# Roots from the sums, a one-step scale, half stores, unread products and a new order in an attention and quantised-layer kernel

## The chip, the cores and the metric

The kernel runs on one core of one Trainium2 chip. The metric is the device time of one execution in microseconds (us). Everything is float32 at the ends; the kernel uses bfloat16 and an eight-bit float inside.

## The reference, cut to what matters

The input `x` is 16 sequences of 512 tokens with 256 features. Two sandwiched layers follow one another:

```python
h  = layernorm(layernorm(x)) * ln_w + ln_b      # eps 1e-5 in both
q, k, v = h @ w_q, h @ w_k, h @ w_v             # 16 heads of 16
q, k = rope(q, theta), rope(k, theta)
t = qk / 4;  a = 1 + t + t*t/2                  # "Taylor softmax"
wv = (a / a.sum(-1)) @ v                        # every token sees every token
x  = x + layernorm(wv @ w_o)

z  = layernorm(x)
s  = max(max|z| over blocks of 32 / 7.5, 1e-30) # one scale for 32 features
zd = nearest_fp6(z / s) * s                     # the weights likewise, once
x  = x + layernorm(zd @ wd.T + bias)
```

Because the polynomial is of second degree, the attention never forms the 512 x 512 matrix: sums over tokens of products of key features with `v` (the tile `psi` holds the features) are multiplied by the same features of the queries.

## The kernel before, in words

The sequence is the unit of work. For each of the 16 sequences the program records some 195 operations: load (`x_load`), double layernorm (`statistics`, `normalised`), transposition, the products with `wk`, `wv_w` and `wq`, rotary embedding, the key features (`coefficients`: DVE, with sums on GpSimd), the query features (`features`: products and ACT squares), the token sums (`token_sums`, L1341), the attention products (`main_part` L1403 and L1422), a DMA round trip that brings the divisors to their places, the division (L1501, for the last two sequences products with a selector and L1539), the product with `wo`, `residual`, the layernorm before the quantiser (`deviations`), the quantiser (`quantised`), the transposition, the product with `wdT` (to which a bf16 product with the bias rows, L993, is added), a second `residual`, and the store.

Every operation is recorded by a `Plan` with its engine, an assumed cost (the first number of each call) and the tiles that it reads and writes. Nothing is emitted then. At the end the literal tuple `ORDER`, 3317 numbers, says in which order the recorded operations are emitted; this is the order of each engine's list, since an engine takes its instructions in order. The order also hands out the buffers: a tile takes a free slot of its class (27 pages, 8 PSUM banks, and so on) when its first operation comes up and gives it back behind its last. So the sequences overlap as the tuple says. Dependences are kept by semaphores that the framework derives.

Five places matter here.

- **Reciprocal root.** `statistics` (17 uses) and `deviations` (54 uses) need 1/sqrt(v + eps) for two or four columns per partition. Six operations: DVE adds eps (L608), ACT takes the root (L763 or L797), DVE takes the reciprocal (L764 or L798), and one Newton step follows: a product (L618) and two combined operations (L628).
- **Scale in `quantised`.** The largest magnitudes `am` of blocks (L858) are divided by 7.5 with a correction: a tensor-scalar (L606), three combined operations (L628), and the lower limit (L606 again). The reciprocal (L869), the products by it and by the scale (L879), and the rounding to eight bits (ACT, L910) follow. A sequence has 32 columns of scales in one piece; the last two sequences have two halves of 16 columns, with the products on DVE instead of GpSimd (`quick`).
- **Stores.** One DMA of 512 KB per sequence from SP's queue. Those of sequences 12 to 15 are the last four numbers of `ORDER`.
- **Sums of squares.** `deviations` lets ACT square 256 columns and accumulate (L784). Only the assumed cost of these operations is touched.
- **Start.** DVE clears the eight banks (L1606), GpSimd sets ones in the first 128 columns of `bias3` (L1604). The weights' quantiser (`exact`) and the rotary table run on DVE in the first 60 us, among the work of the first sequences.

Of the kernel before, what the change touches and what calls it, by code (L numbers as in the profile page):

```python
# [17 lines left out]
ALU = mybir.AluOpType  # L18
# [82 lines left out]
def constants():  # L101
# [40 lines left out]
    8, 3, 0, 93, 65, 9, 16, 4, 1, 5, 7, 2, 6, 333, 94, 19, 20, 95, 66, 21, 132, 67, 130, 22, 23,  # L142
    24, 133, 131, 134, 13, 14, 135, 17, 10, 25, 96, 26, 136, 137, 138, 139, 27, 28, 29, 146, 31,
    140, 147, 30, 148, 338, 149, 97, 68, 69, 32, 12, 141, 142, 143, 150, 151, 144, 145, 48, 33,
    336, 34, 35, 49, 98, 340, 152, 337, 341, 36, 153, 154, 155, 37, 156, 99, 38, 39, 40, 41, 42,
    70, 339, 334, 11, 157, 158, 50, 51, 43, 44, 335, 45, 53, 52, 100, 54, 71, 162, 159, 160,
    161, 46, 47, 125, 165, 55, 342, 343, 72, 73, 101, 163, 164, 166, 56, 57, 76, 167, 15, 126,
    128, 127, 129, 18, 200, 179, 189, 195, 168, 174, 528, 1503, 918, 723, 919, 202, 203, 204,
    1308, 921, 61, 191, 922, 730, 180, 104, 201, 529, 205, 169, 206, 102, 925, 181, 531, 183,
    182, 1113, 344, 731, 345, 59, 74, 533, 103, 346, 347, 207, 530, 532, 348, 1315, 923, 184,  # L150
    208, 187, 245, 240, 170, 106, 192, 924, 177, 535, 105, 190, 350, 246, 185, 209, 349, 188,
    351, 352, 244, 247, 171, 194, 186, 198, 728, 193, 58, 172, 199, 920, 176, 178, 536, 62, 926,
    175, 173, 107, 726, 78, 196, 108, 534, 197, 109, 537, 724, 110, 353, 355, 220, 242, 354,
    356, 243, 235, 395, 236, 237, 239, 241, 63, 221, 215, 238, 222, 216, 223, 357, 224, 225,
    227, 218, 217, 538, 219, 228, 229, 230, 226, 111, 60, 1116, 79, 112, 539, 540, 541, 542, 75,
    113, 725, 1120, 727, 114, 77, 80, 927, 115, 543, 81, 82, 397, 83, 117, 729, 1510, 210, 231,
    233, 213, 214, 64, 234, 232, 360, 928, 211, 212, 251, 249, 248, 250, 252, 84, 732, 362, 85,
    545, 547, 546, 544, 396, 86, 1118, 361, 359, 358, 87, 374, 550, 399, 398, 1698, 254, 1309,
    253, 255, 256, 400, 548, 257, 258, 1504, 375, 376, 1114, 259, 1313, 401, 402, 1705, 549,
    551, 733, 734, 735, 363, 384, 382, 590, 261, 378, 377, 262, 264, 265, 266, 267, 260, 263,  # L160
    268, 592, 365, 929, 386, 552, 554, 591, 553, 440, 379, 116, 442, 403, 435, 364, 380, 383,
    385, 437, 555, 89, 930, 736, 737, 738, 381, 931, 932, 933, 1699, 394, 366, 387, 741, 436,
    404, 88, 441, 438, 390, 369, 594, 593, 595, 269, 90, 118, 410, 569, 557, 571, 556, 388, 570,
    367, 368, 393, 371, 370, 271, 270, 414, 740, 411, 412, 742, 439, 275, 936, 739, 934, 119,
    120, 430, 572, 573, 745, 433, 272, 746, 432, 273, 431, 274, 577, 743, 598, 91, 578, 434,
    413, 373, 276, 372, 935, 277, 415, 416, 417, 92, 418, 419, 391, 278, 389, 279, 392, 280,
    281, 284, 1703, 285, 283, 422, 423, 579, 585, 558, 574, 282, 744, 420, 596, 937, 288, 421,
    581, 121, 1311, 405, 424, 289, 406, 286, 425, 287, 408, 426, 785, 290, 291, 292, 293, 559,
    566, 294, 1506, 295, 428, 764, 940, 409, 427, 429, 407, 296, 597, 786, 787, 122, 297, 599,
    298, 446, 444, 443, 445, 299, 941, 575, 300, 447, 582, 560, 1115, 568, 301, 766, 302, 303,  # L170
    576, 304, 1121, 305, 789, 788, 564, 790, 635, 450, 448, 449, 451, 938, 939, 637, 750, 636,
    123, 791, 625, 452, 453, 768, 306, 1119, 307, 765, 308, 454, 751, 1117, 561, 563, 792, 310,
    980, 747, 793, 309, 627, 626, 629, 628, 311, 749, 752, 748, 630, 314, 312, 632, 124, 580,
    313, 315, 772, 316, 317, 457, 455, 456, 631, 794, 773, 633, 634, 605, 319, 318, 565, 982,
    1122, 1123, 588, 321, 981, 1508, 606, 586, 584, 460, 459, 767, 458, 769, 770, 462, 461, 463,
    464, 983, 984, 465, 320, 607, 608, 587, 567, 1124, 1125, 562, 322, 323, 583, 589, 324, 771,
    468, 467, 466, 469, 470, 471, 325, 610, 612, 472, 609, 613, 611, 614, 615, 616, 326, 473,
    474, 475, 327, 476, 1126, 1127, 753, 479, 480, 478, 477, 483, 481, 330, 755, 329, 617, 618,
    774, 759, 985, 600, 959, 482, 619, 620, 484, 601, 775, 604, 623, 621, 988, 776, 485, 486,
    1701, 961, 328, 487, 331, 488, 777, 489, 490, 491, 1312, 1128, 960, 602, 624, 622, 962, 963,  # L180
    964, 603, 639, 640, 638, 641, 494, 493, 642, 492, 495, 779, 781, 496, 782, 497, 1310, 1314,
    498, 499, 500, 501, 502, 1130, 1131, 1129, 986, 643, 644, 645, 754, 1132, 646, 989, 503,
# [250 lines left out]
def sandwich_kernel(  # L433
# [1169 lines left out]
    with tc.manual_schedule():  # L1603
        nc.gpsimd.memset(bias3.a[:, 0:P], 1.0)  # L1604
        for slot in plan.slots["bank"]:
            nc.vector.memset(slot, 0.0)  # L1606
# [43 lines left out]
```

## Time and profile before

| | |
|---|---|
| Time, median of 3 runs | 612.54 us (610.73 to 616.55) |
| Profiled execution: own time | 612.84 us |
| its span, first to last instruction | 611.0 us |
| mean granted TensorE clock | 0.985 |
| PE busy, weight loads | 569.1 us, 393.8 us |
| DVE, ACT, GpSimd busy | 531.3, 503.8, 181.3 us |
| DMA | 41.27 MB, 68 GB/s on average |

PE is TensorE's matmuls, PEld its weight loads, DVE VectorE, ACT ScalarE, POOL GpSimd, SP the engine that issues most DMAs. Busy time is the union of the instructions' spans. Matmuls are pipelined and their ends are modelled, so 93% busy on PE is not 93% of its peak. The chain of waits goes back from the last instruction, at each step to what released it or to the instruction before it on its engine; its shares tell what the end of the span hung on. A line such as L628 is a helper: all combined operations of DVE on small tiles carry it, and the shape tells them apart.

### The profile page before, as it was taken

The numbers are of one execution on the slowest core, as the hardware profiler recorded it, in microseconds if no ns is written. First come the engines' busy times: TensorE is split into PE (matmuls) and PEld (weight loads), VectorE is DVE, ScalarE is ACT, GpSimd is POOL, SyncE is SP. The second block draws the span as 40 slices with busy tenths as digits, with TensorE's granted clock in tenths as the row PEclk, the third lists the DMA queues.
The fourth block names the chain that finished last, engine by engine and source line by source line (L and its number), as shares of the span: only waits on it lengthen the run. The fifth ranks groups of instructions, "written<-read, shape, count | busy, mean of one in ns | idle before, by whom it ended". The sixth has DMA issues, their size and how long they took to land.

```text
span 611.0 us, 14678 instructions
## 1 busy us (share of the span) xinstructions
PE 569.1 (93%) x5460; PEld 393.8 (64%) x5460; DVE 531.3 (87%) x1346; ACT 503.8 (82%) x1264; POOL 181.3 (30%) x137
## 2 busy tenths in 40 slices
PE   0869999999999999999999999999999999999964
PEld 0636776777757676767866666776767676765543
DVE  7999998899999989888798999888896968997596
ACT  3566699888898888998988878999988897889973
POOL 2310414334333060613343260333327033430200
PEclk9969999999999999999999999999999999999988
DMA  7420410401223141603124212302114020113103
GB/s 221 141 82 18 109 38 19 94 19 21 52 64 89 55 109 48 185 1 98 33 64 134 70 21 74 94 2 63 32 61 139 11 67 36 41 47 89 25 32 104
DMA packets 34968, 41.27 MB, mean 68 GB/s; under 512 B 9808, under 2 KB 27728, under 8 KB 34896
## 3 DMA queue, kind: packets, MB, share of 16 engines
q1 hardware_dynamic: 33344, 38.88, 23.0%
q10 hardware_dynamic: 1552, 1.44, 0.9%
q8 instruction: 43, 0.70, 0.5%
q14 instruction: 29, 0.24, 0.1%
HBM read 17.90 MB, written 9.31 MB: 45 GB/s over the span
## 4 chain that ended last, share of the span: by engine, by line
PE 75%; DVE 12%; ACT 5%; DMA 4%; issue 2%; SPq 1%; DVEq 0%; ACTq 0%
PE bank L985 32%; PE bank L1403 9%; PE bank L1341 9%; PE bank L1128 7%; PE bank L1289 5%; PE bank L924 5%; PE bank L1422 3%; PE bank L1312 3%; DVE psi L1257 2%; PE bank L1049 2%; ACT page L1279 2%; DMA page<-in_L_attn_x_dram 1%; PE bank L993 1%; ACT page L1437 1%; DVE page L1088 1%
## 5 line engine op out<-in xcount | busy, mean ns | idle before, releaser
L1279 ACT ACTIVATE page<-bank 128x512 f32<-128x512 f32 x256 | 145.5, 612 | 10.5 <-PE bank L1289 9.7
L1257 DVE TENSOR_TENSOR psi<-psi 128x896 f32<-128x896 f32 x128 | 142.0, 1127 | 1.0 <-ACT psi L1201 1.0
L1161 POOL TENSOR_TENSOR half<-half,half 128x512 f32<-128x512 f32 x32 | 46.5, 1453 | 189.9 <-DMA half<-half 108.5
L816 ACT ACTIVATE page<-page,small,small 128x256 f32<-128x256 f32 x128 | 70.6, 600 | 7.8 <-DVE small L628 6.4
L1341 PE MATMUL bank<-psi,va 128*17 128x153 f32 x2048 | 72.0, 294 | 2.0 <-DVE half L1143 0.7
L985 PE MATMUL bank<-wdT,page 128*128 128x256 f32 x256 | 66.7, 392 | 2.1 <-ACT page L1571 1.3
L1341 PEld LDWEIGHTS bank<-psi,va 128*17 128x17 f32 x2048 | 57.6, 98 | 17.1 <-issue 9.1
L1188 POOL TENSOR_TENSOR psi<-page,page 128x512 f32<-128x512 f32 x32 | 44.2, 1388 | 74.7 <-PE bank L1341 60.1
L985 PE MATMUL bank<-wk,page 128*128 128x256 f32 x256 | 63.6, 393 | 1.6 <-ACT page L1037 1.6
L784 ACT ACTIVATE squares_room<-bank 128x256 bf16<-128x256 f32 x128 | 50.2, 393 | 15.6 <-PE bank L993 8.3
L879 POOL TENSOR_TENSOR page<-page,small 128x1024 f32<-128x1024 f32 (+1 forms) x16 | 29.4, 1839 | 113.6 <-DVE small L869 57.2
L1128 PE MATMUL bank<-page,wq 128*128 128x256 f32 x256 | 62.7, 390 | 0.2 <-ACT page L1279 0.2
L985 PE MATMUL bank<-wo,page 128*128 128x256 f32 x256 | 60.0, 384 | 2.9 <-ACT page L1279 1.8
L985 PE MATMUL bank<-wv_w,page 128*128 128x256 f32 x256 | 61.1, 384 | 0.2 <-ACT page L1279 0.2
L1403 PE MATMUL bank<-page,page 128*32 128x512 f32 x512 | 58.5, 595 | 0.0
L1017 DVE SCALAR_TENSOR_TENSOR page<-bank,small,page 128x256 f32<-128x256 f32 x128 | 56.3, 473 | 1.4 <-DVE small L628 0.5
L985 PEld LDWEIGHTS bank<-wk,page 128*128 128x128 f32 x256 | 47.8, 194 | 14.1 <-ACT page L1037 2.4
L1128 PEld LDWEIGHTS bank<-page,wq 128*128 128x128 f32 x256 | 47.6, 193 | 13.6 <-issue 2.7
L985 PEld LDWEIGHTS bank<-wo,page 128*128 128x128 f32 x256 | 46.9, 190 | 13.6 <-ACT page L1279 2.6
L985 PEld LDWEIGHTS bank<-wdT,page 128*128 128x128 f32 x256 | 44.9, 194 | 15.2 <-ACT page L972 2.3
L985 PEld LDWEIGHTS bank<-wv_w,page 128*128 128x128 f32 x256 | 46.9, 190 | 10.3 <-issue 2.8
L1289 PE MATMUL bank<-two,sums 32*128 32x512 f32 x512 | 50.7, 451 | 0.4 <-DVE page L1017 0.4
(106 smaller groups left out, 1021.6 us busy)
## 6 DMA issues: line engine op xcount, KB each, us to landing
half<-half SPq DMA_DIRECT2D x64, 128.0 KB
out_dram<-page SPq DMA_DIRECT2D x16, 512.0 KB
page<-in_L_attn_x_dram SPq DMA_DIRECT2D x15, 512.0 KB
page<-rows SPq DMA_DIRECT2D x14, 512.0 KB
page<-page SPq DMA_DIRECT2D x64, 64.0 KB
rows<-rd SPq DMA_DIRECT2D x56, 16.0 KB
page<-in_L_attn_x_dram SPq DMA_DIRECT2D x2, 256.0 KB
rd<-page SPq DMA_DIRECT2D x32, 16.0 KB
```

The lines of the kernel that those rows point to most:

```text
L784: lambda: nc.scalar.activation(squares_room.a, view(src.a), AF.Square, accum_out=sq.a[:, i : i + 1], **known, **({} if mean is None else { ...
L816: lambda: nc.scalar.activation(dst.a[:, first + i], view(src.a), AF.Identity, bias=nb.a[:, i : i + 1], scale=r.a[:, i : i + 1],),
L985: nc.tensor.matmul(pt.a[:, i * D : (i + 1) * D], srcT.a[:, k, c * P : (c + 1) * P], view(k), start=(k == 0), stop=(k == NK - 1 and rows is ...
L1017: lambda: nc.vector.scalar_tensor_tensor(dst.a[:, c], view(src.a), r.a[:, i : i + 1], base.a[:, c], ALU.mult, ALU.add),
L1128: nc.tensor.matmul(pq.a[:, n * D : (n + 1) * D], wq.a[:, k, hf * P : (hf + 1) * P], hT.a[:, k, n * D : (n + 1) * D], start=(k == 0), stop= ...
L1161: lambda: nc.gpsimd.tensor_tensor(cos.a, cos.a, partner.a, ALU.add),
L1188: nc.gpsimd.tensor_tensor(lin().rearrange("p s (i two) -> p s i two", two=2), rc.a[:, hf].rearrange("p c (h i two) -> p (c h) i two", i=HD ...
L1257: nc.vector.tensor_tensor(psi.a[:, s, HD:F_MAIN].rearrange("p s (d i) -> p s d i", i=HD), lin()[:, s].unsqueeze(2).to_broadcast([P, HH, NS ...
L1279: lambda: nc.scalar.activation(dst.a[:, part], pk.a, AF.Square, **bias),
L1289: nc.tensor.matmul(pk[quad].a, sums.a[r, odd], q.a[r, n], start=(n == 0), stop=(n == 1), tile_position=(quad * HS, 0),)
L1341: nc.tensor.matmul(pst.a[j * HS : j * HS + HV, i * F_ALL : (i + 1) * F_ALL], va.a[:, c, (g2 * HH + h8) * HV : (g2 * HH + h8 + 1) * HV], ps ...
L1403: nc.tensor.matmul(banks[g].a[j * HS : (j + 1) * HS], sT.a[:, 0, j, g * HS : (g + 1) * HS], feats[j // 2][0][g % 2, j % 2].a[:, g // 2], s ...
```

## The change

- The reciprocal root becomes a helper `rsqrt`. ACT takes 2 sqrt(v + eps) directly from the variances or sums, with the factor as its scale and a constant tile `eps4` as its bias. DVE computes 4(v + eps) and its reciprocal meanwhile, multiplies by the root, takes the root's reciprocal and adds the two, which is the Newton step's value in another form. Again five DVE operations and one of ACT.
- The quantiser's scale for the sequences is one tensor-scalar (times 1/7.5, lower limit). The weights keep the longer way.
- The stores of the last two sequences go out in halves, each recorded behind its half's residual.
- Twenty groups of six products of ones are recorded on PE (numbers 3247 to 3266). Each writes a bank that nobody reads.
- The assumed costs of the sums of squares are lower (0.472 and 0.602 in place of 0.6 and 0.725).
- `ORDER` is another tuple, with 3267 numbers: 72 operations fewer in the quantiser, two stores and twenty groups more. On PE's list four groups stand ahead of the first transposition; one between the two transpositions of sequence 0, one on either side of its second product with `wv_w`, one behind its first query features, two ahead of its first rest features; then one among sequence 15's features, one behind the transposition of sequence 13's quantised page, one ahead of and two behind the first transposition of sequence 14's, one ahead of its second product with `wdT`, and four behind the last product of sequence 15.

```diff
+    def rsqrt(n, r, name, src, scale, add):
+        v4, inv, sd = (small(f"{name}_{i}", n) for i in ("v4", "inv", "sd"))
+        act(
+            0.205,
+            [V.base(src), eps4],
+            [sd],
+            lambda: nc.scalar.activation(
+                sd.a, V.ap(src), AF.Sqrt, bias=eps4.a[:, add : add + 1], scale=scale
+            ),
+        )
+        V.ts(n, v4, src, scale, 4.0 * EPS * (EPS if add else 1.0), ALU.mult, ALU.add)
+        vec(0.17, [v4], [inv], lambda: nc.vector.reciprocal(inv.a, v4.a))
+        V.tt(n, inv, sd, inv, ALU.mult)
+        vec(0.17, [sd], [v4], lambda: nc.vector.reciprocal(v4.a, sd.a))
+        V.tt(n, r, v4, inv, ALU.add)
...
         if twice:
-            V.ts(n, ve, var, 1.0 + EPS, EPS * EPS, ALU.mult, ALU.add)
+            rsqrt(n, r, "ln", var, 4.0 * (1.0 + EPS), 1)
         else:
-            V.ts(n, ve, var, EPS, None, ALU.add)
-        act(0.205, [ve], [sd], lambda: nc.scalar.activation(sd.a, ve.a, AF.Sqrt))
-        vec(0.17, [sd], [r], lambda: nc.vector.reciprocal(r.a, sd.a))
-
-        V.tt(n, t, r, r, ALU.mult)
-        V.stt(n, t, t, -0.5, ve, ALU.mult, ALU.mult)
-        V.stt(n, r, t, 1.5, r, ALU.add, ALU.mult)
+            rsqrt(n, r, "ln", var, 4.0, 0)
         V.stt(n, nb, mean, -1.0, r, ALU.mult, ALU.mult)
...
-                0.6 if mean is None else 0.725,
+                0.472 if mean is None else 0.602,
...
-        V.ts(n, ve, sq, 1.0 / D, EPS, ALU.mult, ALU.add)
-        act(0.205, [ve], [sd], lambda: nc.scalar.activation(sd.a, ve.a, AF.Sqrt))
-        vec(0.17, [sd], [r], lambda: nc.vector.reciprocal(r.a, sd.a))
-        V.tt(n, t, r, r, ALU.mult)
-        V.stt(n, t, t, -0.5, ve, ALU.mult, ALU.mult)
-        V.stt(n, r, t, 1.5, r, ALU.add, ALU.mult)
+        rsqrt(n, r, "dev", sq, 4.0 / D, 0)
...
-        V.ts(n, s, am, inv, None, ALU.mult)
-        V.stt(n, e, s, -8.0, am, ALU.mult, ALU.add)
-        V.stt(n, e, s, 0.5, e, ALU.mult, ALU.add)
-        V.stt(n, s, e, inv, s, ALU.mult, ALU.add)
-        V.ts(n, s, s, 1e-30, None, ALU.max)
+        if exact:
+            V.ts(n, s, am, inv, None, ALU.mult)
+            V.stt(n, e, s, -8.0, am, ALU.mult, ALU.add)
+            V.stt(n, e, s, 0.5, e, ALU.mult, ALU.add)
+            V.stt(n, s, e, inv, s, ALU.mult, ALU.add)
+            V.ts(n, s, s, 1e-30, None, ALU.max)
+        else:
+            V.ts(n, s, am, inv, 1e-30, ALU.mult, ALU.max)
...
-            residual(y, x2, banks, [2 * c2 + i for c2 in cs for i in range(2)])
-        dma(
-            nc.sync,
-            2.5,
-            [y],
-            [],
-            lambda: out[b].rearrange("(c p) d -> p c d", **kp),
-            lambda: y.a,
-        )
+            cs = [2 * c2 + i for c2 in cs for i in range(2)]
+            residual(y, x2, banks, cs)
+            cut = slice(cs[0], cs[-1] + 1)
+            dma(
+                nc.sync,
+                2.5 if len(cs) == NT else 2.001,
+                [y] if len(cs) == NT else [(y, c) for c in cs],
+                [],
+                lambda cut=cut: out[b].rearrange("(c p) d -> p c d", **kp)[:, cut],
+                lambda cut=cut: y.a[:, cut],
+            )
...
+    ones = bias3
+
+    def warm():
+        pt = bank()
+
+        def emit():
+            row = ones.a[:, 0:P].unsqueeze(1).to_broadcast([P, T // P, P])
+            for _ in range(6):
+                nc.tensor.matmul(
+                    pt.a.rearrange("p (c n) -> p c n", n=P),
+                    ones.a[:, 0:P],
+                    row,
+                    start=True,
+                    stop=True,
+                )
+
+        pe(1.28, [(ones, 0)], [pt], emit)
+
+    for _ in range(20):
+        warm()
+
     with tc.manual_schedule():
         nc.gpsimd.memset(bias3.a[:, 0:P], 1.0)
+        for i in range(2):
+            nc.gpsimd.memset(eps4.a[:, i : i + 1], 4.0 * EPS * (EPS if i else 1.0))
```

The two tuples are left out; the prediction names the places of them that it uses.

## The prediction

> **What bounds the kernel now.** I read the page first: engine totals, clock, chain.
>
> ```profile
> PE 569.1 (93%) x5460; PEld 393.8 (64%) x5460; DVE 531.3 (87%) x1346; ACT 503.8 (82%) x1264; POOL 181.3 (30%) x137
> ...
> PEclk9969999999999999999999999999999999999988
> ...
> PE 75%; DVE 12%; ACT 5%; DMA 4%; issue 2%; SPq 1%; DVEq 0%; ACTq 0%
> ```
>
> Three engines are near full (PE 93%, DVE 87%, ACT 82% of the span), and the chain that ended last passes three quarters of its length through PE. The granted clock is at 9 tenths or more except in the third slice and the last two. So no single engine explains the span: it is PE work plus the places where PE waits. The stretches show where these are.
>
> ```profile
> core 0: us, PE busy (x) PEld busy (x) DVE busy (x) ACT busy (x) POOL busy (x), PEclk, DMA share, GB/s
> 0.00:58.50 58.50, 36.36 (x276) 25.62 (x280) 52.83 (x181) 32.89 (x65) 11.06 (x17) 0.91 0.39 116
> 58.50:553.00 494.50, 490.02 (x4841) 341.22 (x4840) 436.73 (x1008) 428.28 (x1073) 166.38 (x118) 1.00 0.23 62
> 553.00:611.00 58.00, 42.75 (x348) 27.00 (x348) 41.73 (x159) 42.59 (x128) 3.82 (x2) 0.93 0.23 66
> ```
>
> Columns: length, then busy time of PE, PEld, DVE, ACT, POOL with counts, granted clock, DMA. I cut at 58.5 (from here the chain stays mostly on PE) and 553 (from here it leaves it). Adding the chain's pieces by stage gives: **start** 57.8 us, of which PE 14.2 and DVE 26.2, unbroken on DVE from 22.9 to 48.4; **middle** 494.5 us, of which PE 426.6, DVE 35.0, ACT 23.2, DMA 4.4; **tail** 54.1 us, of which PE only 16.9, DVE 14.8, DMA 7.5, ACT 6.9. In the middle the chain is off PE for 68 us, mostly in three passages: 207.7 to 221.1, 325.7 to 358.1 and 483.4 to 497.7. DVE is busy 12.98 of 13.4 us in the first and 30.48 of 32.4 in the second. So the start, these passages and 581 to 592 of the tail are where DVE work counts fully; elsewhere it hides behind PE.
>
> **The parts, and what each is worth.** The sum is against the profiled execution's own 612.84 us (span 611.0, 1.84 around it), 0.3 above the median of 612.54 (610.73 to 616.55).
>
> **1. One-step scale.** Each rescale of sequences loses four small DVE operations. The chain of waits passes through one of them at 215.5 (time, us, what):
>
> ```profile
> 215.51 0.69 DVE small L628
> ...
> 216.22 0.20 DVE small L628
> ```
>
> The groups, by shape (busy, mean ns of one, idle before):
>
> ```profile
> L1279 ACT ACTIVATE page<-bank 128x512 f32<-128x512 f32 x256 | 145.5, 612 | 10.5 <-PE bank L1289 9.7
> ...
> L1279 ACT ACTIVATE page<-bank,shift 128x512 f32<-128x512 f32 x64 | 42.8, 699 | 3.2 <-PE bank L1312 3.0
> ...
> L606 DVE TENSOR_SCALAR small<-small 128x32 f32<-128x32 f32 x42 | 8.7, 206 | 0.5
> L628 DVE SCALAR_TENSOR_TENSOR small<-small,small 128x32 f32<-128x32 f32 x42 | 8.5, 202 | 1.0
> ```
>
> With 32 columns: three at 202 ns and one at 206, 0.81 us; fourteen such, 11.3 us. With 16 columns: three at 172 and one at 158, 0.67 us; four, 2.7 us. Only what stands on the chain counts: in the middle two rescales do (215.5, and 354.7 with the same lines), so 2 x 0.81 = **-1.6**. The cover of the other twelve is PE; were DVE to set the pace all through, it would be -11.3. In the tail, where the quantiser's products run on DVE too, the chain lies on DVE almost unbroken; some of the 2.7 is overlap, so **-2.0** (0 to -2.7).
>
> **2. Reciprocal roots.** 71 of them (L763 x17, L797 x54). DVE work stays equal: before, a tensor-scalar 195, reciprocal 172, product 161 and two of L628 at 167 are 0.86 us; after, 195, twice 172, twice 161, again 0.86. What changes is the chain. The timeline of the last one:
>
> ```profile
> 604.67 0.17 DVE L608 TENSOR_SCALAR small<-small 128x2 f32<-128x2 f32 x1
> ...
> 604.87 0.20 ACT L797 ACTIVATE small<-small 128x2 f32<-128x2 f32 x1 [0.23 <-DVE small L608]
> 605.14 0.15 DVE L798 RECIPROCAL small<-small 128x2 f32<-128x2 f32 x1
> 605.33 0.16 DVE L618 TENSOR_TENSOR small<-small 128x2 f32<-128x2 f32 x1
> 605.52 0.36 DVE L628 SCALAR_TENSOR_TENSOR small<-small,small 128x2 f32<-128x2 f32 x2
> 606.34 0.88 DVE L1017 SCALAR_TENSOR_TENSOR page<-bank,small,page 128x256 f32<-128x256 f32 x2 [0.46 <-DVE small L628]
> ```
>
> From the end of the last sum of squares (604.63) to L628's end the steps follow one another: tensor-scalar, root, reciprocal, product, two more. In the change the root starts on ACT's own sums, with no DVE step first, while DVE does v4 and its reciprocal; behind the root come product, reciprocal, sum. From 604.67: root 0.20 plus 0.09 (below), then three steps at the 0.19 by which these starts follow one another, gives 605.6 where it was 605.88: -0.28. About five are in series in the tail (two roots of sequence 14, three of 15): **-1.4** (0 to -3.4, all twelve). In the middle these lines hold about 2 us of the chain, less 22%: **-0.4**. ACT's 8.5 us idle for L608 goes; behind it queue the evictions that free PE's banks. The DVE operation that now waits is the product with the root, with the rest of DVE's list behind it, as L798 waits today (6.2 us).
>
> The root now takes its bias from a tile. No row shows a root both ways; nearest are L1279 with and without a tile bias, 699 and 612 (+87 ns), and L784, 511 and 393 (+118, with another source too). I take 0.09 of 0 to 0.118: 71 x 0.09 = 6.4 us of ACT. ACT has 4.7% of the middle's chain: **+0.3**; if ACT set the pace, +6.4. The Trainium skill, ScalarE: Activation LUTs, section "What ACT_TABLE_LOAD costs", states that each pointer operand adds about 93 ns; by that figure, an estimate, ACT gains 6.6 us and the sum moves by nothing visible.
>
> **3. Stores in halves.** Only the last two sequences. The last 512 KB store issues at 607.25 and the span ends 3.75 later. Half of it goes earlier; the fixed part remains. Gain 0 to 1.9, and two issues more on SP at a median 0.49 each, ahead of the last one if DVE finishes early (at worst +1.0). I take **-0.7**, nearer to no gain, since small stores have a landing time too.
>
> **4. Unread products.** 20 groups of six 512-column bf16 matmuls. The chain shows 256 columns of bf16 (L993) at 0.11 us, so 0.22 each, 1.32 a group, 26.4 in all. By the new list four come ahead of the first transposes, six among the start's products, six in the tail's, and four behind the last real product. PE is busy 36.4 of 58.5 us at the start and 42.8 of 58 in the tail, so 22.1 and 15.3 us of room hide them; where the operands behind a group are already there, it costs its 1.32 whole. Gain: the first eight L985 matmuls take 3.78 us and the same eight later 1.73, but that is ahead of a DVE passage that is full anyway (18.07 of 18.10 from 30.5 to 48.6); in the tail the clock is 0.93 for 42.8 us of PE, 16.9 of it on the chain: 1.2 at most. I take **-0.5** (+21.1 for sixteen groups to -3.2).
> The Trainium skill, TensorE: Matmul & The Clock Gate, section "What's actually happening", says PE starts at half clock and is released after some 3.4 us of activity. Taken by that rule alone the first matmuls would save 2.05 us, and the sum would be 2.05 lower; the 3.78 against 1.73 agrees with the rule, though the granted clock of the stretch from 15.3 to 23 us reads 1.00.
>
> **5. The new order.** Start: ahead of the first token sums the new list leaves out five 256-wide products and one mask of the weights' quantiser (0.43 x3, 0.41 x2, 0.29: 2.4 us) and has four small operations more (0.66): **-1.7**, since DVE is unbroken there. That work comes later, under PE. In the middle a list can open or close passages: the three are 60.1 us together, another like the first would cost 13.4. One thing can be read from the lists: the wait of L1501 for the DMA round trip (9.6 us of DVE idle). Work by the kernel's own costs between the last av product and L1501 is at least 13 us of DVE before and 16 after. I take a third of the 9.6, **-3.0** (+13.4 to -60).
>
> **Sum:** -1.7 -1.6 -2.0 -1.4 -0.4 +0.3 -0.7 -0.5 -3.0 = -11.0, so **601.8 us**, PE remaining the bound.
>
> **Rivals.**
> *A, DVE was the pace-setter.* For: DVE 87%, and two of three passages full of it. Against: the chain has 7% of the middle on it. Then the rescale gives its whole 11.3 instead of 1.6, and L1501's 9.6 go instead of 3.0: 601.8 - 9.7 - 6.6 = 585.5.
> *B, the middle takes nothing.* For: PE alone has 426.6 of 494.5; what DVE saves and the start postpones is met again. Only the tail gains: 612.8 - 2.0 - 1.4 - 0.7 = 608.7.
> *C, ACT sets the pace.* For: 82% busy, its evictions free the banks. Against: 4.7% of the middle's chain. 601.8 - 0.3 + 6.4 = 607.9. The page on ScalarE named above gives the same direction.
> *D, the unread products stand in the way* (slower). Place: PE's list, where six groups lie between products of the start and six in the tail, and PE takes them in order. Each whose followers are ready costs 1.32. For: the two just ahead of sequence 0's rest features feed ACT, and three stand around sequence 14's first turned block. Against: 22.1 and 15.3 us of room. From nine groups on (11.5 / 1.32 = 8.7) the change loses; at all sixteen, 601.8 + 0.5 + 21.1 = 623.4.
>
> **Chances.** My forecast 0.50 (its own range 594 to 607), A 0.18, B 0.14, C 0.06, D 0.12. A measurement of this kernel tells about 1% from no change (606.4 to 618.7). Faster: 0.46 + 0.18 + 0.04 of B + 0.03 of C = 0.71; same: 0.04 + 0.10 + 0.03 + 0.02 of D = 0.19; slower: 0.10. The range goes to A's time and into D: 586 to 617.
>
> **What would show it.** Right: DVE about 14 us less busy (517), L606 and L628 with 32 columns fewer by 14 and 42; root rows near 0.3 us and no ACT wait for a tensor-scalar; token sums of sequence 0 starting near 47 instead of 48.6; the tail beginning (last main products of sequence 15 done) some 6 us sooner; the last store about 3 us before the end; PE busy up by up to 26 while its chain share does not rise. Wrong: PE waits behind groups of ones with data ready (D); ACT pieces growing in the chain (C); the chain off PE in the middle for 68 us still (B) or under 50 (A).

## Result and profile after

The changed kernel takes 607.39 us (median of 17 runs, 604.46 to 609.22), the kernel before, run beside it, 613.30 (17 runs, 609.48 to 616.55): a ratio of 0.9904 (0.9884 to 0.9923). A later comparison of the same pair on one chip, the first of the last four experiments below, gave 606.13 against 614.35, 0.9855 (0.982 to 0.9889). The change is faster by 1.0 to 1.4%, 6 to 9 us, where 11 were forecast. Both intervals exclude no change, though 607.4 by itself lies within the 606.4 to 618.7 that the prediction could not tell from none. The profiled execution took 607.85 us with a span of 605.8.

The page of the profile after: busy times, granted clock in 40 slices, and the shares of the chain that ended last.

```profile
PE 588.0 (97%) x5580; PEld 405.1 (67%) x5580; DVE 534.5 (88%) x1274; ACT 510.1 (84%) x1264; POOL 185.4 (31%) x139
...
PEclk8889999999999999999999999998999999999999
...
PE 69%; DVE 17%; ACT 7%; DMA 3%; issue 2%; POOL 1%; SPq 0%; ACTq 0%; DVEq 0%
```

PE is now busy 97% of the span instead of 93%, but that is the unread products (without them it is 564.6 us, third experiment below, where it was 569.1 before); the chain has less PE on it than before (69%, it was 75) and more DVE (17%, it was 12). DVE's busy time has not fallen: 534.5 us where it was 531.3 and 517 was forecast.

The stretches, cut at the same two points as before (length, then busy time of PE, PEld, DVE, ACT, POOL, granted clock, DMA share):

```profile
core 0: us, PE busy (x) PEld busy (x) DVE busy (x) ACT busy (x) POOL busy (x), PEclk, DMA share, GB/s
0.00:58.50 58.50, 48.34 (x344) 30.19 (x348) 52.68 (x189) 33.82 (x65) 11.92 (x20) 0.91 0.39 121
58.50:553.00 494.50, 489.13 (x4838) 343.94 (x4830) 443.05 (x949) 434.31 (x1076) 169.67 (x118) 1.00 0.23 64
553.00:605.80 52.80, 50.55 (x404) 30.95 (x402) 38.75 (x137) 42.00 (x125) 3.83 (x2) 1.00 0.19 52
```

In the first row DVE is nearly full again (52.7 of 58.5 us); the second is as long as before by its cut, and PE has 489.1 us of it; the tail is 52.8 us instead of 58.0, at a clock of 1.00 instead of 0.93. A cut that moves with the work is the end of a sequence's last attention product. Sequence 0 ends at 61.9 us (before 63.2), sequence 14 at 550.4 (552.3), so the span divides like this:

| | before | after | forecast gain | gain |
|---|---|---|---|---|
| start, to the end of sequence 0 | 63.2 | 61.9 | 1.7 | 1.3 |
| middle, to the end of sequence 14 | 489.1 | 488.5 | 4.7 | 0.6 |
| tail | 58.7 | 55.4 | 4.6 | 3.3 |

The forecast column adds the terms of the sum: in the middle 1.6 + 0.4 - 0.3 + 3.0, in the tail 2.0 + 1.4 + 0.7 + 0.5.

Four groups of before that the prediction didn't show (busy, mean ns of one | idle before, its releasers):

```profile
L1170 DVE TENSOR_TENSOR two<-half,two 128x512 fp32r<-128x512 f32 x32 | 23.1, 725 | 0.5 <-ACT two L1165 0.5
...
L1501 DVE TENSOR_TENSOR page<-page,page 128x1024 f32<-128x1024 f32 x14 | 19.0, 1355 | 9.6 <-DMA page<-page 3.8 <-DMA page<-rows 3.1 <-DMA half<-half 2.5
...
L618 DVE TENSOR_TENSOR small<-small 128x4 f32<-128x4 f32 x57 | 9.1, 161 | 1.0
...
L797 ACT ACTIVATE small<-small 128x4 f32<-128x4 f32 x42 | 8.8, 211 | 7.7 <-DVE small L608 7.3
```

The groups that answer to these and to those of the prediction, after:

```profile
L1179 DVE TENSOR_TENSOR two<-half,two 128x512 fp32r<-128x512 f32 x32 | 30.4, 953 | 2.0 <-ACT two L1174 2.0
...
L617 DVE TENSOR_TENSOR small<-small,small 128x4 f32<-128x4 f32 x114 | 23.7, 213 | 2.9 <-ACT small L745 1.3
...
L1510 DVE TENSOR_TENSOR page<-page,page 128x1024 f32<-128x1024 f32 x14 | 20.5, 1466 | 6.6 <-DMA page<-rows 4.8 <-issue 1.4 <-DMA page<-page 0.3
...
L745 ACT ACTIVATE small<-small,eps 128x4 f32<-128x4 f32 x42 | 12.5, 301 | 0.4
...
L607 DVE TENSOR_SCALAR small<-small 128x4 f32<-128x4 f32 x42 | 8.4, 201 | 21.2 <-ACT squares_room L795 21.2
...
L607 DVE TENSOR_SCALAR small<-small 128x32 f32<-128x32 f32 x14 | 3.3, 235 | 0.1
```

The quantiser's L628 rows with 32 columns are gone and one tensor-scalar with 32 columns and L607 is left at x14, as forecast. A root with its bias from a tile takes 301 ns, where 211 was the row before; ACT no longer waits for a tensor-scalar (0.4 us of idle before these 42 roots, 7.7 in the row before). But three rows are longer by their mean, with the same work: L1179 takes 953 ns (before 725), L617 with four columns 213 (161 for its like before), and L1510 1466 (1355). The timeline of the last root, to be set beside that of before:

```profile
600.67 0.30 ACT L745 ACTIVATE small<-small,eps 128x2 f32<-128x2 f32 x1
600.77 0.16 DVE L607 TENSOR_SCALAR small<-small 128x2 f32<-128x2 f32 x1
600.97 0.17 DVE L750 RECIPROCAL small<-small 128x2 f32<-128x2 f32 x1
601.24 0.16 DVE L617 TENSOR_TENSOR small<-small,small 128x2 f32<-128x2 f32 x1
601.31 0.16 DVE L752 RECIPROCAL small<-small 128x2 f32<-128x2 f32 x1
601.51 0.16 DVE L617 TENSOR_TENSOR small<-small,small 128x2 f32<-128x2 f32 x1
601.77 0.88 DVE L1026 SCALAR_TENSOR_TENSOR page<-bank,small,page 128x256 f32<-128x256 f32 x2
```

The root starts 0.03 us after the last sum (ACT, 600.64) and ends at 600.97; the two DVE operations that need no root run beside it. The last product behind it ends at 601.67, 1.03 us after the sum; it was 1.25.

### The profile page after: what moved, and what is told of

It is laid out like the page before. It is cut to its first block, busy times and chain, and to the rows that moved or that the text cites. A ratio compares the mean times of both kernels' runs of the same rounds, so it can differ in the third digit from the quotient of the medians.

```text
span 605.8 us, 14857 instructions
## 1 busy us (share of the span) xinstructions
PE 588.0 (97%) x5580; PEld 405.1 (67%) x5580; DVE 534.5 (88%) x1274; ACT 510.1 (84%) x1264; POOL 185.4 (31%) x139
## 4 chain that ended last, share of the span: by engine, by line
PE 69%; DVE 17%; ACT 7%; DMA 3%; issue 2%; POOL 1%; SPq 0%; ACTq 0%; DVEq 0%
PE bank L994 28%; PE bank L1350 9%; PE bank L1412 7%; PE bank L1137 6%; PE bank L1298 6%; PE bank L933 4%; DVE psi L1266 3%; PE bank L1623 2%; PE bank L1321 2%; PE bank L1431 2%; PE bank L1058 2%; DVE page L1026 2%; ACT squares_room L795 2%; DVE half L1152 2%; DVE page L1097 2%
## 5 line engine op out<-in xcount | busy, mean ns | idle before, releaser
L1266 DVE TENSOR_TENSOR psi<-psi 128x896 f32<-128x896 f32 x128 | 142.7, 1128 | 0.1
L1170 POOL TENSOR_TENSOR half<-half,half 128x512 f32<-128x512 f32 x32 | 48.0, 1501 | 182.1 <-DMA half<-half 120.9
L888 POOL TENSOR_TENSOR page<-page,small 128x1024 f32<-128x1024 f32 (+1 forms) x16 | 28.3, 1774 | 124.1 <-DVE small L878 70.0
L1197 POOL TENSOR_TENSOR psi<-page,page 128x512 f32<-128x512 f32 x32 | 45.6, 1432 | 64.9 <-PE bank L1350 25.5
L994 PE MATMUL bank<-wdT,page 128*128 128x256 f32 x256 | 64.3, 382 | 0.5 <-ACT page L981 0.5
L994 PE MATMUL bank<-wk,page 128*128 128x256 f32 x256 | 62.1, 388 | 0.6 <-ACT page L1288 0.5
L994 PE MATMUL bank<-wv_w,page 128*128 128x256 f32 x256 | 59.6, 380 | 0.1
L1026 DVE SCALAR_TENSOR_TENSOR page<-bank,small,page 128x256 f32<-128x256 f32 x128 | 56.1, 473 | 1.1
L1298 PE MATMUL bank<-two,sums 32*128 32x512 f32 x512 | 48.5, 446 | 4.1 <-ACT sums L576 2.6
```

What stands on the lines that cost most here:

```text
L994: nc.tensor.matmul(pt.a[:, i * D : (i + 1) * D], srcT.a[:, k, c * P : (c + 1) * P], view(k), start=(k == 0), stop=(k == NK - 1 and rows is ...
L1026: lambda: nc.vector.scalar_tensor_tensor(dst.a[:, c], view(src.a), r.a[:, i : i + 1], base.a[:, c], ALU.mult, ALU.add),
L1170: lambda: nc.gpsimd.tensor_tensor(cos.a, cos.a, partner.a, ALU.add),
L1197: nc.gpsimd.tensor_tensor(lin().rearrange("p s (i two) -> p s i two", two=2), rc.a[:, hf].rearrange("p c (h i two) -> p (c h) i two", i=HD ...
L1266: nc.vector.tensor_tensor(psi.a[:, s, HD:F_MAIN].rearrange("p s (d i) -> p s d i", i=HD), lin()[:, s].unsqueeze(2).to_broadcast([P, HH, NS ...
L1298: nc.tensor.matmul(pk[quad].a, sums.a[r, odd], q.a[r, n], start=(n == 0), stop=(n == 1), tile_position=(quad * HS, 0),)
```

## Experiments

The theory I began with: order and edits each bring a part, and the parts add up. Its rivals: the order alone brings the gain; and TensorE paces both lists, so that only its own work and waits count. "List" below is the order of operations; "old" is that of the kernel before, "new" that of the change. Each ratio is to the kernel before on the same chip.

**Edits in the old list.** Roots and one-step scale of the change, whole stores, no unread products.

```diff
 ORDER = (            # the old list, renumbered for the new operations
...
-    for _ in range(20):
-        warm()
```

> The changed arithmetic (roots, one-step scale) in the list of before: no groups of ones, whole stores. Theory 1 (the new list gives back what the edits save, because more of DVE's operations with both operands in SBUF run beside GpSimd and stretch: DVE busy was 534.5 us after the change although some 14 us of work had left it): here DVE is 517 to 522 us busy and the time is 604 to 607 us. Theory 2 (DVE's savings in the middle hide under PE, only start and tail gain, and these by the list): 609 to 612 us, the tail's savings alone.

Measured: 615.46 us against 616.48, 0.9989 (0.9968 to 1.001). DVE was busy 521.1 us, ten less, and nothing came of it: the middle is 488.5 us long (489.1 before), the tail 60.8 (58.7). Both expectations are missed (604 to 607 and 609 to 612 us). In the old list VectorE's work is covered, in the tail too.

**The new list alone.** Before's roots, scale and stores in the new list; each tensor-scalar of a root stands just ahead of the root, since the new list has no place for it.

```diff
 ORDER = (            # the new list, renumbered for the old operations
...
-    def rsqrt(n, r, name, src, scale, add):
+    ...              # tensor-scalar, root, reciprocal and Newton step as before
```

> The arithmetic of before (Newton step, corrected scale, whole stores, no ones) in the new list. Theory 1: DVE busy rises to 545 to 552 us (the stretch without the saving) and the time is 613 to 622 us, not faster than before. Theory 2: the list brings what was gained at the start and behind the last attention; 607 to 610 us.

Measured: 677.94 us, 1.0993 (1.0965 to 1.1021). The chain of this run:

```profile
PE 42%; DVE 34%; ACT 11%; issue 8%; DMA 2%; POOL 2%; ACTq 0%; DVEq 0%; SPq 0%; POOLq 0%
```

PE has 42% of the chain where it had 75. Both expectations are far too low (622 us at most). The list isn't better by itself: it is made for the edits, and without them it is 10% slower than the kernel before.

**The change without its unread products.**

```diff
-    for _ in range(20):
-        warm()
```

> The changed kernel without the twenty groups of ones; all else and the order of the rest the same. If they are free and useless: 605 to 608 us, as the changed kernel. If they stand in the way (the prediction's rival D): faster, 598 to 603. If they help by the clock at the start and in the tail: slower by 1 to 4 us, with the granted clock of the last 20 us back at 0.86 to 0.93.

Measured: 607.41 us, 0.9855 (0.9819 to 0.9891), the very ratio that the change itself had in its later comparison. The twenty groups bring and cost nothing that shows within the 0.4% (some 2 us) by which each interval reaches to either side.

**The change with the long scale.** The corrected division is put back for the sequences, all at the place of the one step.

```diff
-        if exact:
+        if True:
             V.ts(n, s, am, ...
```

> The changed kernel with the corrected scale of before in the sequences' quantiser (four more small DVE operations in each of 18 rescales, 14.0 us of DVE), put right behind the first. Theory 1 (DVE sets the pace in the new list: the chain has 83 us of DVE in the middle where it had 35): slower than the changed kernel by 6 to 14 us. Theory 2 (hidden under PE but for the tail): by 1 to 4 us.

Measured: 619.26 us, 1.0033 (1.0007 to 1.0058), with DVE at 550.3 us. Against the change that is 1.3 to 1.8%, 8 to 11 us, for 16 us of VectorE's time, as theory 1 had it. In the old list the same operations, together with the roots, were worth nothing. So the new list has little slack on VectorE.

**Without the bias products, in both lists.** 64 products of 256 columns go; they follow one another at 0.11 us, so PE has 7 us less to do.

```diff
-                if rows:
-                    nc.tensor.matmul(
-                        pt.a[:, i * D : (i + 1) * D], rows.a[:, 0:P], ...
```

> The changed kernel without the bf16 products that add the bias (128 of 256 columns, in the trace 64 records at 0.11 us on the chain, so 7 to 14 us of PE); the output lacks the bias. Theory P (PE's own list sets the pace of the middle, and so DVE's savings bring nothing there): 6 to 12 us faster than the changed kernel, 595 to 602. Theory Q (in the new list DVE sets the pace, since GpSimd stretches its operations): less than 3 us faster, 604 to 608.

> The kernel before without the bias products; the output lacks the bias. Theory P: 6 to 12 us faster than before. Theory Q speaks of the new list alone: here the same 6 to 12, since the saving in DVE work brought nothing in the old list. If neither engine but the latency of the chain sets the pace of both lists: under 3 us.

Measured: new list 602.75 us, 0.9819 (0.9794 to 0.9845); old list 612.87, 0.9996 (0.9971 to 1.0021). PE's busy time fell by 6.4 us in the new list and by 2.2 in the old. At the end of the kernel that gave 2 to 5 us in the new list, between the two theories, and nothing in the old, where both theories had 6 to 12 and only the third case, that no engine's own work sets the pace, had under 3. In the profile of the old list the middle is 487.4 us long (489.1 before) and the tail 62.0 at a clock of 0.89 (58.7 at 0.93), so in that execution the tail took back what the middle gave. "TensorE alone paces both" falls: in the old list neither ten microseconds off VectorE nor these products off TensorE move the end; in the new list each counts. Two engines that hold each other up by turns would look like this; that reading is not shown.

**Most of GpSimd's work left out, in both lists.** The rotary sums on GpSimd shrink to 16 columns, the quantiser's products to one, and the feature products to two slots.

```diff
-            lambda: nc.gpsimd.tensor_tensor(cos.a, cos.a, partner.a, ALU.add),
+            lambda: nc.gpsimd.tensor_tensor(cos.a[:, 0:16], cos.a[:, 0:16], partner.a[:, 0:16], ALU.add),
...
-                lambda: on.tensor_tensor(V.ap(dst), V.ap(a), V.ap(b), ALU.mult),
+                lambda: on.tensor_tensor(*((x if quick or exact else x[:, 0:1]) for x in (...)), ALU.mult),
```

> The changed kernel with most of GpSimd's work left out: the sum of the rotary halves on 16 of 512 columns, the quantiser's two products on one block in place (first fourteen sequences), the half products of the features on 2 of 32 groups; the sums of key features stay whole. Theory Q: the DVE operations that were stretched come back towards their undisturbed length (subtraction into the rounded pair 953 to some 700 ns), DVE busy falls to 515 to 522, and the time by 6 to 12 us, more than in the old list. Theory P: the DVE operations get shorter too, but the time falls by under 4 us.

> The kernel before with the same part of GpSimd's work left out. Theory Q: DVE busy falls from 531 to some 522 and the time by 0 to 4 us, less than the new list gains. Theory P: under 4 us, as in the new list.

Measured: new list 598.51 us, 0.9765 (0.9743 to 0.9788); old list 608.19, 0.9929 (0.9901 to 0.9957). The pages' busy lines, new list first:

```profile
PE 584.6 (98%) x5580; PEld 403.2 (68%) x5580; DVE 499.9 (84%) x1274; ACT 509.1 (85%) x1264; POOL 79.6 (13%) x141
```

```profile
PE 568.1 (94%) x5460; PEld 393.7 (65%) x5460; DVE 513.2 (85%) x1346; ACT 503.3 (83%) x1264; POOL 78.1 (13%) x141
```

GpSimd gives up about 105 us in each. VectorE, whose instructions are the same in number and nearly all in size, falls by 34.6 us in the new list (534.5 to 499.9) and by 18.1 in the old (531.3 to 513.2). The row of L1179 falls from 953 ns to 767, that of L617 with four columns from 213 to 151. So GpSimd's work lengthens VectorE's, and twice as much in the new list. In time the cut is worth 5 to 9 us in the new list against the change, and 4 in the old: nearer to theory Q. What happens is seen in the change's own trace near 411 us. DVE (start, us, what):

```profile
409.07 1.08 DVE L617 TENSOR_TENSOR small<-small,small 128x4 f32<-128x4 f32 x1
...
411.10 1.86 DVE L617 TENSOR_TENSOR small<-small,small 128x4 f32<-128x4 f32 x1
...
412.96 0.76 DVE L607 TENSOR_SCALAR small<-mean 128x4 f32<-128x4 f32 x1
413.63 0.17 DVE L605 TENSOR_SCALAR small<-small 128x32 f32<-128x32 f32 x1
413.72 0.86 DVE L1026 SCALAR_TENSOR_TENSOR page<-bank,small,page 128x256 f32<-128x256 f32 x2
```

GpSimd in the same stretch:

```profile
408.86 1.27 POOL L1170 TENSOR_TENSOR half<-half,half 128x512 f32<-128x512 f32 x1 [13.30 <-DMA half<-half]
410.78 2.16 POOL L888 TENSOR_TENSOR page<-page,small 128x1024 f32<-128x1024 f32 x1 [0.64 <-DVE small L878]
412.90 0.79 POOL L1250 TENSOR_TENSOR psi<-psi 128x256 f32<-128x256 f32 x1
```

A product of four columns takes 0.13 us elsewhere. At 409.07 it takes 1.08 and ends at 410.15, with GpSimd's L1170 (410.13); at 411.10 it takes 1.86 and ends at 412.96, with GpSimd's L888 (412.94); the tensor-scalar behind it ends with L1250. VectorE stands still for 1.7 us there. Summed over all VectorE operations that ran beside a GpSimd operation, the time above the quick quarter of their own shape is some 25 us before and 47 after (28 for the edits in the old list, 48 for the new list alone, so it comes with the list). With GpSimd's work cut, 5 are left in the old list and 11 in the new. Of the 47, some 9 are L1179, 8 L617, 7 L1266, 6 L607. What is taken as undisturbed moves these sums by about 1 us. Operations that read a PSUM bank (L1152, L1097) keep their 0.68 us beside GpSimd, and reciprocals their 0.17.

The Trainium skill, SBUF — State Buffer, section "SBUF: two separate sides", says that VectorE and GpSimd share one pair of SBUF ports, given for a whole instruction to whichever of the two starts first, if VectorE's has two SBUF inputs or runs in a two-port mode; the other waits. The trace agrees, and so does the immunity of the PSUM readers. All eight small products of L617 that took over 0.3 us end 0.02 us behind a GpSimd instruction. A large operation still has its own work to do then: all nine L1179 that were held end 0.55 us behind one, such as the one from 62.39 to 64.15 beside a GpSimd product from 62.30 to 63.60. GpSimd is held in its turn: of its 32 products of L1250, 20 take 0.78 to 0.80 us, and the 12 longer ones (1.24 to 1.77) each end 0.65 us behind a VectorE operation. Which mode the small tensor-scalars ran in, no view here tells.

What the 1.86 us cost on PE, and what the granted clock did behind it:

```profile
414.63 0.49 PE L1321 MATMUL bank<-two,sums 64*128 64x512 f32 x1 [0.55 <-DVE page L1026]
416.67 0.73 PE L1321 MATMUL bank<-two,sums 64*128 64x512 f32 x3 [1.55 <-DVE page L1026]
```

```profile
415.00:417.00 2.00, 0.45 (x3) 0.29 (x3) 2.00 (x6) 0.00 (x0) 1.60 (x1) 1.00 0.00 0
417.00:419.00 2.00, 2.00 (x9) 1.42 (x7) 2.00 (x5) 1.79 (x4) 0.00 (x0) 0.80 0.00 0
419.00:421.00 2.00, 2.00 (x9) 1.62 (x8) 2.00 (x4) 1.93 (x4) 0.00 (x0) 0.50 0.07 17
421.00:423.00 2.00, 2.00 (x11) 1.86 (x10) 2.00 (x4) 1.09 (x3) 0.00 (x0) 0.85 0.28 49
```

The delayed product is the end of a root whose residual step (L1026) frees the banks for L1321. PE waits 0.55 and 1.55 us, and then its clock is granted at 0.80, 0.50 and 0.85 in three stretches of 2 us: by estimate another 1.7 us lost (2 x 0.20 + 2 x 0.50 + 2 x 0.15). This happens in some executions only. In the next experiment the same kernel's profiled run had one wait of 1.22 us there, no fall of the clock, and a span of 602.6.

**The change again, beside three variants on one chip.**

```diff
 (no edit)
```

> The changed kernel itself, as the measure for the three runs beside it. Every theory: 0.990 of the kernel before (0.988 to 0.992), some 607 us; DVE busy 534, and the same 2.1 us wait of PE before L1321 near 415 us, with the granted clock at 0.78 to 0.80 for the 8 us behind it.

Measured: 606.13 us (604.42 to 608.64), 0.9855 (0.982 to 0.9889): 0.5% better than expected, and in its profile without the fall of the clock. The two of its six runs with a mean clock of 0.989 took 608.4 and 608.6 us, the four at 0.992 to 0.994 604.4 to 607.1. One such fall goes with some 3 us of the spread between runs (that it is this place is seen in the two profiles alone); one profile must not be read to the microsecond.

**The old roots in the new list**, all else as in the change.

```diff
-            lambda: nc.scalar.activation(sd.a, V.ap(src), AF.Sqrt, bias=eps4.a[:, add : add + 1], scale=scale),
+        V.ts(n, ve, src, scale / 4.0, EPS * ..., ALU.mult, ALU.add)
+        act(0.205, [ve], [sd], lambda: nc.scalar.activation(sd.a, ve.a, AF.Sqrt))
...
```

> The change with the old roots alone: a tensor-scalar on VectorE ahead of each ScalarE root, and the Newton step behind it, in the new order. Putting back the long scale cost 1.3%, putting back everything 9.9%. Theory 'the costs of the parts add up': the roots are what is left of the 9.9%, about 8%, so some 655 us. Theory 'each stall is small until they fall together': a root behind a tensor-scalar delays one chain of 0.2 to 0.5 us, 42 or so times, of which the new order can hide about half: 1 to 3% over the change, 613 to 625 us.

Measured: 660.17 us, 1.0733 (1.0699 to 1.0768), 8.9% over the change beside it (660.17 / 606.13). The parts nearly add up here: 8.9% and the long scale's 1.3 to 1.8 make 10.2 to 10.7%, and the list alone, against the change, is 11.0 to 11.5% slower (the 9.9 in the expectation is against the kernel before). My count of 0.2 to 0.5 us a root was far too small. DVE does hardly more (540.5 us). The rows of its root on ACT and of its tensor-scalar on DVE:

```profile
L740 ACT ACTIVATE small<-small 128x4 f32<-128x4 f32 (+1 forms) x71 | 14.8, 211 | 22.6 <-DVE small L607 19.9 <-DMA lnb<-in_L_attn_ln_b_dram 2.5
```

```profile
L607 DVE TENSOR_SCALAR small<-small 128x4 f32<-128x4 f32 (+3 forms) x72 | 14.2, 201 | 65.6 <-ACT squares_room L786 65.3
```

ACT waits 19.9 us for the tensor-scalar, and DVE stands 65.3 us with the tensor-scalar at the head of its list, waiting for ACT's sums (24.7 over the same forms in the change). Both queues are taken in order, so each waits for the other in turn with everything else behind. In the middle PE's idle time grows to 30.1 us and its clock falls:

```profile
63.80:596.00 532.20, 502.07 (x4770) 350.60 (x4770) 440.52 (x934) 425.14 (x1063) 170.79 (x117) 0.97 0.22 59
```

Part of this is my placing of the tensor-scalar just ahead of the root: a list searched for these roots may place it better, which was not run. That this list, with the tensor-scalar placed so, needs roots that start on ACT alone is shown; what such roots are worth by themselves is not.

**One place of the list altered.** The delayed product of 411 us and the four residual steps that need it go ahead of the reciprocal that starts GpSimd's product.

```diff
-    ... 2635, 2021, 1850, 2160, ... 2022, 2308, 1851, 2636, ... 1853, 1852, 2473, 1855, 2292, 2824, 1854,
+    ... 2635, 2021, 1850, 1851, 1853, 1852, 1855, 1854, 2160, ... 2022, 2308, 2636, ... 2473, 2292, 2824,
```

> The change with one place of its order altered: the last multiply of the eighth sequence's second-norm root and the four residual steps that need it are issued ahead of the reciprocal that starts a GpSimd product. In the changed kernel that multiply took 1.86 us instead of 0.13 and ended with the GpSimd product, the first residual step came 2.4 us later, PE stood 2.1 us before L1321, and the granted clock was 0.78 to 0.80 for 8 us. Theory 'a GpSimd operation holds up VectorE operations with two operands in SBUF': the multiply takes 0.13 to 0.2 us, the wait and the lower clock go, 3 to 3.7 us less than the run of the change beside it (603 to 604 us, 0.994 of it). Rival 'VectorE's whole load sets the pace': the work is only shifted, and the time stays within 1 us.

Measured: 607.81 us (605.37 to 609.12), 0.9868 (0.9833 to 0.9903), 1.7 us above the change beside it and within its spread. DVE and PE at that place:

```profile
410.39 0.16 DVE L617 TENSOR_TENSOR small<-small,small 128x4 f32<-128x4 f32 x1
...
412.97 1.86 DVE L627 SCALAR_TENSOR_TENSOR small<-mean,small 128x4 f32<-128x4 f32 x1
...
415.52 0.68 DVE L1152 TENSOR_TENSOR half<-bank,ropeT 128x512 f32<-128x512 f32 x1
```

```profile
415.01 0.73 PE L1321 MATMUL bank<-two,sums 64*128 64x512 f32 x4
417.51 2.93 PE L994 MATMUL bank<-wk,page 128*128 128x256 f32 x6 [1.76 <-DVE half L1152]
```

The product takes 0.16 us and L1321 doesn't wait any more, as expected. But now L627, also with two small operands in SBUF, is caught by the same GpSimd product for 1.86 us, L1152 comes late behind it, and PE waits 1.76 us one group later. The hold-up moved on with the work. The theory is right about the operation and wrong about the time; the rival's "only shifted" fits this place, but that VectorE's whole load sets the pace is not shown by it.

**The change with uncorrected roots.** ScalarE's root and one reciprocal, at the places of the root and of its reciprocal in the new list.

```diff
-        V.ts(n, v4, src, scale, 4.0 * EPS * (EPS if add else 1.0), ALU.mult, ALU.add)
-        vec(0.17, [v4], [inv], lambda: nc.vector.reciprocal(inv.a, v4.a))
-        V.tt(n, inv, sd, inv, ALU.mult)
-        vec(0.17, [sd], [v4], lambda: nc.vector.reciprocal(v4.a, sd.a))
-        V.tt(n, r, v4, inv, ALU.add)
+        vec(0.17, [sd], [r], lambda: nc.vector.reciprocal(r.a, sd.a))
```

> The change with the correction of its roots left out: ScalarE's root and one reciprocal, without the tensor-scalar, the other reciprocal and the two products (the correction of the root is not computed). VectorE then does about 190 small operations less, 30 to 36 us of its 534. Theory 'VectorE with its hold-ups sets the pace of the new order': as much as the GpSimd cut gave, 6 to 9 us less, 598 to 601 us. Rival 'TensorE's own work sets the pace of the middle': only the idle time left there, 5.4 us, and the clock's 1.6 can be had, so 2 to 4 us less, 603 to 605 us.

Measured: 601.22 us (600.39 to 602.06), 0.9772 (0.9745 to 0.98): the fastest version that computes the whole layer, apart from that correction. It is 4.9 us under the change beside it, between the two expectations. 284 instructions go, not 190 (four for each of 71 roots), and VectorE falls by 35.5 us to 498.2:

```profile
PE 585.3 (98%) x5580; PEld 402.6 (67%) x5580; DVE 498.2 (83%) x990; ACT 508.9 (85%) x1264; POOL 186.8 (31%) x139
...
PE 85%; DVE 7%; ACT 4%; DMA 2%; issue 1%; SPq 1%; POOL 0%; ACTq 0%; DVEq 0%
```

Only 4.9 of 35.5 us arrive, and the chain that is left is PE's to 85%. The middle of five kernels, each from its own end of sequence 0 to that of sequence 14: before, the change as profiled first, the change again, with uncorrected roots, and with most of GpSimd's work left out.

```profile
63.20:552.30 489.10, 484.69 (x4774) 339.80 (x4774) 431.33 (x993) 424.86 (x1066) 164.98 (x117) 1.00 0.23 61
```

```profile
61.90:550.40 488.50, 483.13 (x4772) 342.08 (x4770) 437.72 (x940) 429.05 (x1064) 169.12 (x117) 1.00 0.24 64
```

```profile
60.90:547.10 486.20, 481.52 (x4770) 340.95 (x4770) 436.87 (x940) 428.67 (x1064) 168.87 (x117) 1.00 0.24 65
```

```profile
62.40:545.10 482.70, 480.93 (x4770) 339.95 (x4770) 412.39 (x735) 428.07 (x1066) 170.53 (x117) 1.00 0.24 65
```

```profile
61.40:541.30 479.90, 478.85 (x4775) 339.55 (x4770) 406.43 (x941) 428.35 (x1065) 70.41 (x117) 1.00 0.24 65
```

Length minus PE's busy time is 4.4, 5.4, 4.7, 1.8 and 1.1 us. PE's busy time itself is 484.7, 483.1, 481.5, 480.9 and 478.9 us. It bounds the stage closely, but it is no fixed floor: with the same products it differs by 6 us between the first row and the last, and no run here tells why.

## Why the prediction came out as it did

The side was right, and the range held the time; the likeliest case was 5.6 us too low, and the measured 607.4 lies at rival B ("the middle takes nothing", 608.7), though not with B's sign: the chain is off PE in the middle for 133 us, not for 68 still. Of the signs, the counts of instructions, the roots and the last store came as written, but VectorE's busy time didn't, and the main products of sequence 15 end 2.2 us sooner (570.6, before 572.8), not 6.

**What failed: the middle, the terms -3.0 (part 5) and -1.6 (part 1).** I took 4.7 us out of a stage from the chain's 68 us off PE, and got 0.6 (2.9 in the second profile). The second view that I showed had the bound: PE busy 490.0 of 494.5 us, so 4.5 us idle, and 4.7 us would have needed every one of PE's waits to go. The chain of waits goes through DVE wherever DVE released something late, but PE had other products to do meanwhile, and those 68 us were no room. After the change it is off PE for those 133 us and the stage is no longer. The wait that the -3.0 was taken from did shrink as forecast, from 9.6 us of DVE idle to 6.6; it wasn't on the way to the end. In reading a stage, the idle time of its fullest engine is the first bound on the gain; I divided the chain instead. Why only 0.6 of these 4.5 us came is less certain: the runs with less VectorE time in the new list (uncorrected roots, GpSimd's work cut) leave PE idle for 1.8 and 1.1 us, so in the change itself VectorE still held PE up.

**Part 1's scale** left as many instructions as forecast, and in the new list it is worth 1.3 to 1.8%, far more than 3.6 us; in the old list, with the roots, 0.1%. **Part 2's roots** went as forecast one by one (the end of the last root 0.22 us sooner after its sum, forecast 0.28; 0.09 us longer on ACT, as taken; ACT's wait gone). (The written steps, 0.20 + 0.09 + 3 x 0.19 from 604.67, give 605.53 and 0.35 sooner; 605.6 also holds the 0.07 us between root and reciprocal.) In the new list their form decides 8.9%. So the sum's error of method is that it priced edits on the old list's chain and added the order behind: the roots and the scale are worth nearly nothing alone (0.9989) and the list alone loses 10%. Only the pair gains, and that a sum of such terms came within 1% of the time is partly luck.

**VectorE's busy time** was forecast at 517 and is 534.5. The work did shrink: without the time lost beside GpSimd it is some 506 us before (531.3 - 25) and 487 after (534.5 - 47), 19 us less. The hold-ups gave 22 us back. The working had no term for this, though a line that it showed was a hold-up: the L628 of 0.69 us at 215.51, with a mean of 0.20 for its shape, beside a GpSimd operation from 215.34 to 216.13. Rival A's 585.5 (DVE paces) lacks the same term.

**Part 3's half stores:** the last store is issued 3.1 us before the end instead of 3.75, a gain of 0.65 where 0.7 was taken. This was read from the trace and not run alone. **Part 4's unread products** were put at -0.5, and no effect shows; rival D did not occur. With them the tail takes 55.4 us at a clock of 1.00, without them, in the same list, 56.8 at 0.95; the whole time is no different. **Part 5's start:** sequence 0's token sums begin at 44.2 us (48.6 before, forecast 47), yet sequence 0 ends only 1.3 us sooner. **The tail** gave 3.3 us of 4.6; in the old list the roots and the scale gave it nothing (60.8 us), so apart from the stores this too is the pair's doing.

**Still open:** how much of the new list's loss beside GpSimd costs time. GpSimd's cut gave 0.9 to 1.4% in the new list and 0.7% in the old, but it also shortens GpSimd's own answers; a version that removes the collisions alone was not found.

## What to carry to other kernels

Hold what a stage can gain against the idle time of its fullest engine before you price edits from the chain of waits: here 4.5 us, where the chain showed 68. It is a first bound, not a strict one: leaving out GpSimd's work in the new list made the middle 9.2 us shorter than before, as PE's busy time fell too. Don't price an order and the edits it was made for as a sum; an order fitted to one form of an operation lost 9% here with another form of about equal work. And when VectorE and GpSimd both work on SBUF, count collisions as VectorE time: a 0.13 us operation can cost 1.86.

## What the runs showed of the hardware that was not expected

- VectorE operations with two operands in SBUF, and small tensor-scalars, are held until a GpSimd operation beside them ends, most of the time: some 25 us of 531 before, 47 of 534 after. A small one ends 0.02 to 0.06 us behind it. GpSimd operations are held by VectorE's likewise (L1250: 0.79 us, or up to 1.77). Operations with a PSUM operand (0.68 us) and reciprocals (0.17) are not held.
- The granted clock fell to 0.50 behind waits of 0.55 and 1.55 us that were 0.5 us apart, and behind one of 1.76 us, but not behind one of 1.22. The Trainium skill, TensorE: Matmul & The Clock Gate, section "What's actually happening", puts the fall behind an idle window of about 3.4 us; here less idle time was enough. The length alone doesn't decide: without the unread products, the clock stays at 1.00 behind a wait of 2.72 us at 583.4.
- Products ahead of the real ones don't keep the clock up across a pause. PE rows of the unread products, and the stretch in which the second group lies:

```profile
1.46 7.17 PE L1623 MATMUL bank<-bias 128*128 128x512 bf16 x24 [1.46 <-DVE bank L1641]
...
15.57 2.77 PE L1623 MATMUL bank<-bias 128*128 128x512 bf16 x6
...
28.44 1.46 PE L1623 MATMUL bank<-bias 128*128 128x512 bf16 x6
```

```profile
12.00:18.00 6.00, 3.33 (x10) 1.83 (x11) 4.58 (x26) 2.97 (x7) 0.00 (x0) 0.50 1.11 329
```

Twenty-four products take 7.17 us from 1.46; after a pause of some 6 us six of them take 2.77 at a granted clock of 0.50, and 1.46 later. The start's clock is 0.91, as before.
